# A two-layer graph network on one core: the first phase in one fixed order, and its buffers and loads shifted

## The chip, the cores and the metric

The kernel runs on one core of one Trainium2 chip. The metric is the device time of one execution in microseconds, as the median of the runs shown. All data are 32-bit floats. The engines are named as in the profile: PE is TensorE (PEld its weight loads), DVE is VectorE, ACT is ScalarE, POOL is GpSimd; SP is SyncE, which computes nothing and issues DMAs. ACT can issue DMAs too.

## The reference

The input is x, 128 graphs of 128 nodes with 256 features, and adj, one 128 x 128 matrix per graph. Cut to what is computed:

```python
# layer 0
norm  = (adj.sum(-1) + 1e-6) ** -0.5
f_hom = adj @ ((x @ theta) * norm) * norm
gate  = sigmoid(x @ W_t + b_t)
x1    = layernorm(x + elu(gate * f_hom + (1 - gate) * (x @ W_h)))
# layer 1
h      = relu(bn1(conv1d(x1^T, conv1_w)))              # one tap
x_conv = relu(bn2(conv1d(h, conv2_w, pad=8)) + x1^T)^T # 17 taps along the nodes
s      = x1 @ w_se.T + b_se                            # 3 coordinates per node
A      = exp(-|s_n - s_m|^2)
x_nmp  = A @ relu(x1 @ w_msg.T + b_msg)
out    = layernorm(x1 + GRU([x_conv, x_nmp], x1))
```

## The kernel before, in words

The work has three phases. The first phase computes layer 0 and, along the way, the first convolution and its analysis into 136 coefficients per channel and graph. It also turns the 17 taps of conv2_w into the same coefficients. The second phase multiplies coefficients of h and of the taps (L740, L753), and the third computes the rest of layer 1, mostly the products of the GRU (L999). The change touches only the first phase.

The first phase goes over 64 tiles of J = 2 graphs, in rounds t = -1 to 63. In round t several tiles are in work at once: l1_turn transposes x1 of tile t-2 on TensorE (L305) and VectorE copies it into the tile x1T (L309); l0_project multiplies x of tile t with theta and W_h (f_ps, L341) and with W_t (gate_ps, L346); between the two graphs of it come l0_gate of tile t-1 (L381 to L384) and l1_analyse of tile t-3 (coef_ps, L431); l0_elu of tile t-1 (L390, L391, statistics) and l0_norm (x1, L292) follow; l1_front of tile t-2 is the first convolution (conv_ps, L411) and h (L415 to L419); l0_turn of tile t+1 makes xT (a VectorE transpose of xb, L315) and the row sums of adj (L321, L323); l0_mix of tile t is L367 and L372.

SyncE issues the round's DMAs: l1_store of tile t-2 (x1 to x1_d at L423, x1T to x1T_d at L424), load_x of tile t (L134), load of tile t+2 (four DMAs of xb at L122, one of adjT at L129), in rounds 2 to 8 two small DMAs into TL (leftover_table, L275), and then what belongs to the taps.

The taps come in two kinds of units. Of the 32 units of w_unit, each takes 4 x 17 taps, loaded by w_load in four DMAs (L141) into one of two wt buffers; TensorE makes four products (w_ps, L447), ScalarE copies them into four wo buffers (L451), and w_store (L456) sends them to w_d in the next round. The 19 units of v_unit take the leftover rows: v_load (L471) brings up to 119 rows into one of two vt buffers, one product (wl_ps, L478), one copy on VectorE (L482), and v_store (L489) in the next round. The dicts units and units_v (L530 to L532) say in which round a unit is: before, units of the first kind are in rounds 2, 3, 5, 7, 9 and so on to 63, and those of the second kind in even rounds from 10 to 62. The v_load of the unit after next is issued at the end of the unit's own round.

What sets the order: manual_schedule(engines=...) keeps the instructions of the named engines in the order in which the code issues them; for the other engines a planner chooses the order from the dependencies and its own estimates. Before, each round has a manual_schedule of its own (L537): for TensorE alone up to t = 2, and for TensorE, SyncE, VectorE and ScalarE from t = 3 on. The end of the phase (L605 to L634) has another one. Tiles of one tag in a pool take turns in its buffers: x1T has one, x1, x, xb, hom, het and gate have two, adjT has four, xT one. An instruction that writes into a buffer waits until all that used the buffer's former tile is done, DMAs included.

At the start (L144 to L170) SyncE loads tile 0 and a third of w0 (the three weights of layer 0), and ScalarE issues the other two thirds, b_t, and eight small loads of the batch norms' vectors. Each third takes four DMAs of 64 KB. WARM = 7 matmuls without use (L529) run on TensorE before the first tile comes. VectorE computes a table of cosines (L209 to L223) in the rounds 0 and 1, and TensorE's program waits in places for VectorE there.

Of the kernel before, what the change touches and what calls it, by code (L numbers as in the profile page):

```python
# [26 lines left out]
M = L  # L27
# [7 lines left out]
def gnn_layers_kernel(ctx: ExitStack, tc: tile.TileContext, a: dict, out: bass.AP):  # L35
# [10 lines left out]
    nc = tc.nc  # L46
    x, adjT = a["x"], a["adjT"]
    NB = x.shape[0]
    NP = NB // J
# [43 lines left out]
    conv1_w = acon.tile([P, NC, D + CO], F32, tag="conv1_w", name="conv1_w")  # L93
    shift1 = acon.tile([P, D], F32, tag="shift1", name="shift1")
    K, Q = 32, P // 32
    WARM = 7
    NW = 2
    vt = [taps.tile([P, 2, D], F32, tag=f"vt{i}", name=f"vt{i}") for i in range(2)]
    wt = [taps.tile([P, 2, D], F32, tag=f"wt{i}", name=f"wt{i}") for i in range(NW)]


# [34 lines left out]
    NU = QF = P // Q  # L136

    def w_load(u):
        v = a["conv2_wT"].rearrange("(c f) t o -> f t c o", c=NC)
        for r in range(Q):  # L140
            nc.sync.dma_start(wt[u % NW][K * r : K * r + TAPS], v[r * QF + u])  # L141
# [112 lines left out]
    def way_back():  # L254

        AL = setup.tile([P, P // ML, ML], F32, tag="AL", name="AL")
        nc.vector.tensor_copy(AL, A[:, P:M].unsqueeze(1).to_broadcast([P, P // ML, ML]))
        nc.vector.memset(TL, 0.0)

        for t in vt:  # L260
            nc.vector.memset(t[96:], 0.0)
# [207 lines left out]
    def v_load(v):  # L469
        f, n = v_set(v)  # L470
        nc.sync.dma_start(  # L471
            vt[v % 2][0 : n * TAPS],
            a["conv2_wT"].rearrange("(c f) t o -> (f t) c o", c=NC)[f * TAPS : (f + n) * TAPS],
        )

    def v_unit(v):
        pl = bank(f"wl_ps_{v}")
        nc.tensor.matmul(  # L478
            pl, lhsT=TL, rhs=vt[v % 2].rearrange("p c o -> p (c o)"), start=True, stop=True
        )  # L480
        ol = s_v[v] = taps.tile([ML * FS, NC * D], F32, tag="wl", name=f"wl_o_{v}")
        nc.vector.tensor_copy(ol, pl[0 : ML * FS])  # L482
# [44 lines left out]
    warm = bank("warm_ps")  # L527
    for _ in range(WARM):
        nc.tensor.matmul(warm[:, 0:P], lhsT=ones, rhs=ones, start=True, stop=True)  # L529
    units = {2 + u * (NP - 3) // (NU - 1): u for u in range(NU)}  # L530
    rest = [t for t in range(3 + FS, NP - 1) if t not in units]
    units_v = {rest[v * (len(rest) - 1) // (NV - 1)]: v for v in range(NV)}  # L532
    hstack = ExitStack()
    H = None
    E = mybir.EngineType
    for t in range(-1, NP):
        with tc.manual_schedule(engines={E.PE, E.SP, E.DVE, E.Activation} if t > 2 else {E.PE}):  # L537

            def on(q, work):
                if 0 <= q < NP:  # L540
                    work(q)

            def between():
                on(t - 1, l0_gate)
                on(t - 3, l1_analyse)

            def beside():
                on(t - 1, l0_elu)

            on(t - 2, l1_turn)  # L550
            l0_project(t, between, beside) if t >= 0 else between()
            on(t - 1, l0_norm)
            if t == 0:
                norms = batch_norms()
                next(norms)
                l0_turn(1)
                table(AT2, (node, lag))

                cos, sin = T[:, 2:M:2], T[:, 3:M:2]
                both = setup.tile([P, M // 2 - 1], F32, tag="both", name="both")  # L560
                nc.vector.tensor_sub(both, sin, cos)
                nc.vector.scalar_tensor_tensor(sin, sin, -1.0, cos, ALU.mult, ALU.subtract)
                nc.vector.tensor_copy(cos, both)
            on(t - 2, l1_front)
            on(t - 2, l1_store)
            if t >= 0:
                load_x(t)
            if t + 2 < NP:
                if 2 <= t + 2:
                    load(t + 2)  # L570
                if 0 <= t < 2:
                    w_load(t)
                if 2 <= t < 2 + FS:
                    leftover_table(t - 2)
                if FS <= t < 2 + FS:
                    v_load(t - FS)
            else:
                m_load(t + 2 - NP)
            if t - 1 in units:
                w_store(units[t - 1])  # L580
                if units[t - 1] + NW < NU:
                    w_load(units[t - 1] + NW)
            if t - 1 in units_v:
                v_store(units_v[t - 1])
            if t != 0:
                on(t + 1, l0_turn)
            if t == 3:
                nc.scalar.dma_start(w_msg, a["w_msgT"].rearrange("(c p) e -> p c e", p=P))
                nc.scalar.dma_start(b_msg, a["L1_gnn_b_msg"].partition_broadcast(P))
            if t == 1:  # L590
                next(norms, None)
                way_back()
                sctx.close()
                hpool = hstack.enter_context(tc.tile_pool(name="hpool", bufs=1))
                H = hpool.tile([P, NC, M, NB], F32, tag="H", name="H")
            on(t, l0_mix)
            if t in units_v:
                v_unit(units_v[t])
                if units_v[t] + 2 < NV:
                    v_load(units_v[t] + 2)  # L600
            if t in units:
                if t + 1 < NP:
                    w_unit(units[t])
# [511 lines left out]
```

## Time and profile before

| what | value |
|---|---|
| median of 3 runs | 2004.11 us (2003.17 to 2006.05) |
| the profiled execution: its own time | 2004.55 us |
| its span, first to last instruction | 2002.8 us |
| first phase | from 0 to about 691 us |
| second and third phase | about 691 to 875 us, 875 us to the end |
| TensorE busy | 1974.8 us of the span |
| granted TensorE clock, mean | 0.994 |

A line of the table of stretches gives the stretch in us from the span's start, its length, and each engine's busy time and number of instructions in it, then the granted clock, the mean busy share of the 16 DMA engines and GB/s. A line of a timeline gives start, duration, engine, line of the code, operation, what it writes and reads, its shape and number; in brackets stands how long the engine was idle just before, and what ended that. Engine names with a q (SPq, ACTq) are the engine's issuing part; the duration of a DMA there is that of its issue, not of the transfer. When a transfer has landed is read from the record of the semaphore that it raises.

### The profile page before, as it was taken

How to read it: one execution, taken by the hardware profiler on the slowest of the kernel's cores; microseconds unless marked ns; L12 is line 12 of the kernel's file. 1: busy time of each engine (PE TensorE's matmuls, PEld its weight loads, DVE VectorE, ACT ScalarE, POOL GpSimd, SP SyncE). 2: the span in 40 equal slices, each digit the busy share in tenths (PEclk: the TensorE clock that was granted, in tenths of full speed). 3: DMA queues.
4: the chain of work that ended last, by engine and by line, in shares of the span. 5: the costliest groups of instructions: out<-in, count | busy, mean ns of one | idle time of the engine just before them, and what ended most of it. 6: DMA issues, size and time to landing. Idle time of an engine off the chain costs nothing.

```text
span 2002.8 us, 26505 instructions
## 1 busy us (share of the span) xinstructions
PE 1974.8 (99%) x8437; PEld 1348.1 (67%) x8437; DVE 1447.2 (72%) x2867; ACT 746.7 (37%) x1488; POOL 630.5 (31%) x855
## 2 busy tenths in 40 slices
PE   8999999999999999999999999999999999999997
PEld 5566666666666788876666666666666666666664
DVE  7678888888888654467777777767767776776766
ACT  3566666666666511122232222322222222222222
POOL 2111111111111255544243243424334343433331
PEclk9899999999999999999999999999999999999999
DMA  4566555566565689983212122212222221221100
GB/s 120 173 195 189 181 184 184 186 187 195 177 191 181 219 315 329 324 267 91 66 62 81 59 67 67 81 58 70 75 65 64 70 81 48 80 76 37 46 23 21
DMA packets 239568, 259.72 MB, mean 130 GB/s; under 512 B 84406, under 2 KB 174278, under 8 KB 239430
## 3 DMA queue, kind: packets, MB, share of 16 engines
q1 hardware_dynamic: 232982, 252.26, 39.3%
q10 hardware_dynamic: 6448, 5.78, 1.0%
q8 instruction: 68, 1.11, 0.2%
q14 instruction: 70, 0.57, 0.1%
HBM read 153.10 MB, written 104.86 MB: 129 GB/s over the span
## 4 chain that ended last, share of the span: by engine, by line
PE 94%; DVE 3%; DMA 1%; ACT 1%; issue 0%; POOL 0%; SPq 0%; ACTq 0%; POOLq 0%; DVEq 0%
PE g_ps L999 43%; PE f_ps L341 10%; PE y_ps L740 5%; PE msg_ps L876 5%; PE conv_ps L411 5%; PE gate_ps L346 5%; PE nmp_ps L932 3%; PE conv_ps L840 3%; PE coef_ps L431 3%; PE z_ps L753 3%; PE mix_ps L367 3%; PE x1T_ps L305 2%; PE w_ps L447 2%; PE conv_ps L847 1%; PE wl_ps L478 1%; PE adj_ps L321 1%
## 5 line engine op out<-in xcount | busy, mean ns | idle before, releaser
L341 PE MATMUL f_ps<-w,xT 128*128 128x512 f32 x512 | 246.3, 604 | 2.7 <-DVE xT L315 2.7
L174 POOL TENSOR_SCALAR rstd_b<-mv_b 128x2 f32<-128x2 f32 (+1 forms) x65 | 12.6, 194 | 529.5 <-DVE mv_b L283 529.5
L958 ACT ACTIVATE o<-o 128x1024 f32<-128x1024 f32 (+1 forms) x65 | 67.8, 1044 | 268.1 <-DVE o L1035 263.6
L999 PE MATMUL g_ps<-t_h,sh 128*128 128x384 f32 x384 | 156.9, 490 | 0.0
L999 PE MATMUL g_ps<-t_c,sc 128*128 128x384 f32 x384 | 155.3, 486 | 0.0
L999 PE MATMUL g_ps<-t_m,sm 128*128 128x384 f32 x384 | 155.3, 486 | 0.0
L292 ACT ACTIVATE y<-y,nb_b,rstd_b 128x256 f32<-128x256 f32 x128 | 70.0, 593 | 219.3 <-DVE nb_b L290 219.3
L346 PEld LDWEIGHTS gate_ps<-w,xT 128*128 128x128 f32 x512 | 98.4, 192 | 69.6 <-issue 61.9
L174 POOL TENSOR_SCALAR rstd_a<-mv_a 128x2 f32<-128x2 f32 x64 | 12.3, 192 | 400.7 <-DVE mv_a L283 400.7
L341 PEld LDWEIGHTS f_ps<-w,xT 128*128 128x128 f32 x512 | 89.5, 194 | 66.5 <-issue 66.4
L346 PE MATMUL gate_ps<-w,xT 128*128 128x256 f32 x512 | 132.6, 382 | 0.0
L1032 POOL TENSOR_TENSOR u<-u,p 128x512 f32<-128x512 f32 x63 | 79.9, 1267 | 162.7 <-DVE p L1016 162.7
L740 PE MATMUL y_ps<-wb,H 128*128 128x256 f32 x544 | 128.4, 379 | 0.8 <-issue 0.8
L411 PE MATMUL conv_ps<-conv_w,x1T 128*128 128x259 f32 x512 | 122.5, 381 | 0.0
L748 POOL TENSOR_TENSOR ws<-wb 128x512 f32<-128x512 f32 x67 | 92.5, 1381 | 89.7 <-PE z_ps L753 50.3
L350 ACT ACTIVATE hom<-f_ps,norm 128x256 f32<-128x256 f32 x128 | 60.7, 474 | 158.7 <-PE f_ps L341 158.7
L740 PEld LDWEIGHTS y_ps<-wb,H 128*128 128x128 f32 x544 | 103.3, 190 | 15.0 <-POOL ws L748 1.0
L876 PE MATMUL msg_ps<-w_msg,cx1T 128*128 128x256 f32 x480 | 108.7, 379 | 0.0
L999 PEld LDWEIGHTS g_ps<-t_c,sc 128*128 128x128 f32 x384 | 73.0, 190 | 50.9
L999 PEld LDWEIGHTS g_ps<-t_m,sm 128*128 128x128 f32 x384 | 73.0, 190 | 50.9
L411 PEld LDWEIGHTS conv_ps<-conv_w,x1T 128*128 128x128 f32 x512 | 97.1, 190 | 14.7 <-ACT w_o L451 0.2
L999 PE MATMUL g_ps<-w_hhT_w,cx1T 128*128 128x384 f32 x256 | 105.1, 492 | 0.0
(217 smaller groups left out, 4431.6 us busy)
## 6 DMA issues: line engine op xcount, KB each, us to landing
wb<-w_d SPq DMA_DIRECT2D x68, 512.0 KB
w_d<-w_o SPq DMA_DIRECT2D x128, 256.0 KB
y_d<-yb SPq DMA_DIRECT2D x68, 256.0 KB
xb<-in_x SPq DMA_DIRECT2D x256, 64.0 KB
x<-in_x SPq DMA_DIRECT2D x64, 256.0 KB
cx1T<-x1T_d SPq DMA_DIRECT2D x64, 256.0 KB
yt<-y_d SPq DMA_DIRECT2D x32, 512.0 KB
cx<-x_d SPq DMA_DIRECT2D x32, 512.0 KB
```

Of the source, the lines that this page charges most:

```text
L292: nc.scalar.activation(dst[:, q, :], src[:, q, :], AF.Identity, bias=nb[:, q : q + 1], scale=rstd[:, q : q + 1],)
L341: nc.tensor.matmul(pf, lhsT=xT[:, c, nodes(j)], rhs=w0[:, c, 0 : 2 * D], start=(c == 0), stop=(c == NC - 1),)
L346: nc.tensor.matmul(pg[:, j * D : (j + 1) * D], lhsT=xT[:, c, nodes(j)], rhs=w0[:, c, 2 * D : 3 * D], start=(c == 0), stop=(c == NC - 1),)
L350: nc.scalar.activation(hom[:, j, :], pf[:, 0:D], AF.Copy, scale=norm[:, j : j + 1])
L367: nc.tensor.matmul(pm[:, j * D : (j + 1) * D], lhsT=adjT_[:, j, :], rhs=hom[:, j, :], start=True, stop=True,)
L411: nc.tensor.matmul(ph[:, 0 : D + CO], lhsT=s["x1T"][:, c, nodes(j)], rhs=conv1_w[:, c, :], start=(c == 0), stop=(c == NC - 1),)
L740: nc.tensor.matmul(py[:, blk, :], lhsT=coefs(blk if k == 0 else 2 * k + 1 - blk, c), rhs=w[:, blk, c, :], start=(c == 0), stop=(c == NC - 1),)
L748: nc.gpsimd.tensor_tensor(ws, w[:, 0], w[:, 1], ALU.add)
L876: nc.tensor.matmul(pm[:, j * D : (j + 1) * D], lhsT=x1T[:, c, nodes(q)], rhs=w_msg[:, c, :], start=(c == 0), stop=(c == NC - 1),)
L958: nc.scalar.activation(rz, rz, AF.Tanh, scale=0.5)
L999: nc.tensor.matmul(pg[:, lo : lo + 3 * P], lhsT=s[f"f{kind}"][i][:, pr, :], rhs=factors[kind][i], start=(k == 0), stop=(k == 2), skip_grou ...
L1032: nc.gpsimd.tensor_tensor(u4, u2, p5, add)
```

## The change

- The rounds from t = 3 to 63 and the end of the phase stand in one manual_schedule for TensorE, SyncE, VectorE and ScalarE. The body of a round becomes a function, a_round. Rounds -1 to 2 stay as they were.
- x1T has two buffers instead of one, adjT three instead of four, vt one instead of two.
- v_load of the next unit is issued in the round after a unit, behind its v_store, and not two units ahead; v_load(1) in round 8 goes.
- w_load takes K = 32 consecutive rows for each of the four parts, where it took the 17 taps that are used; only the last part of the last unit takes 17. The products still read 17 rows.
- The units of the first kind are in rounds 2, 4, 6 to 32 and then 33, 35 to 63; the second kind goes to odd rounds from 11 to 31 and even rounds from 34 to 62.
- Each third of w0 comes in two DMAs of 128 KB over 128 partitions, not four of 64 KB over 32.
- WARM is 14. A small tanh on ScalarE (first) is issued after the first loads.

```diff
-    WARM = 7
+    WARM = 14
...
-    vt = [taps.tile([P, 2, D], F32, tag=f"vt{i}", name=f"vt{i}") for i in range(2)]
+    vt = taps.tile([P, 2, D], F32, tag="vt", name="vt")
...
-        s["adjT"] = io.tile([P, J, P], F32, tag="adjT", name=f"adjT_{p}")
+        s["adjT"] = io.tile([P, J, P], F32, tag="adjT", bufs=3, name=f"adjT_{p}")
...
-        v = a["conv2_wT"].rearrange("(c f) t o -> f t c o", c=NC)
+        v = a["conv2_wT"].rearrange("(c f) t o -> (f t) c o", c=NC)
         for r in range(Q):
-            nc.sync.dma_start(wt[u % NW][K * r : K * r + TAPS], v[r * QF + u])
+            n = TAPS if u == NU - 1 and r == Q - 1 else K
+            nc.sync.dma_start(wt[u % NW][K * r : K * r + n], v[(r * QF + u) * TAPS :][:n])
...
-        for q in range(Q):
-            (nc.sync if j == 2 else nc.scalar).dma_start(
-                w0[q * K : (q + 1) * K, :, j * D : (j + 1) * D],
-                a[name][2 * K * q : 2 * K * (q + 1)].rearrange("(c i) e -> i c e", i=K),
-            )
+        v = a[name].rearrange("(q c i) e -> c q i e", q=Q, c=NC)
+        for c in range(NC):
+            (nc.sync if j == 2 else nc.scalar).dma_start(w0[:, c, j * D : (j + 1) * D], v[c])
...
+    first = setup.tile([P, G], F32, tag="first", name="first")
+    nc.scalar.activation(first, neg_half, AF.Tanh)
...
-        s["x1T"] = wk.tile([P, NC, J * P], F32, tag="x1T", name=f"x1T_{p}")
+        s["x1T"] = wk.tile([P, NC, J * P], F32, tag="x1T", bufs=2, name=f"x1T_{p}")
...
-    units = {2 + u * (NP - 3) // (NU - 1): u for u in range(NU)}
+    units = {2 + 2 * u - 2 * u // NU: u for u in range(NU)}
...
-    for t in range(-1, NP):
-        with tc.manual_schedule(engines={E.PE, E.SP, E.DVE, E.Activation} if t > 2 else {E.PE}):
...
+    def a_round(t):
...
-            if FS <= t < 2 + FS:
-                v_load(t - FS)
+            if t == FS:
+                v_load(0)
...
         if t - 1 in units_v:
             v_store(units_v[t - 1])
+            if units_v[t - 1] + 1 < NV:
+                v_load(units_v[t - 1] + 1)
...
         if t in units_v:
             v_unit(units_v[t])
-            if units_v[t] + 2 < NV:
-                v_load(units_v[t] + 2)
...
+    for t in range(-1, 3):
+        with tc.manual_schedule(engines={E.PE}):
+            a_round(t)
     with tc.manual_schedule(engines={E.PE, E.SP, E.DVE, E.Activation}):
+        for t in range(3, NP):
+            a_round(t)
         last = NP - 1
```

More of the change, by code (lines that the diff above doesn't have):

```diff
@@ L258, in way_back @@
         nc.vector.memset(TL, 0.0)
-        for t in vt:
-            nc.vector.memset(t[96:], 0.0)
+        nc.vector.memset(vt[96:], 0.0)
         back = setup.tile([P, 1], F32, tag="back", name="back")
@@ L471, in v_load @@
         nc.sync.dma_start(
-            vt[v % 2][0 : n * TAPS],
+            vt[0 : n * TAPS],
             a["conv2_wT"].rearrange("(c f) t o -> (f t) c o", c=NC)[f * TAPS : (f + n) * TAPS],
@@ L478, in v_unit @@
         nc.tensor.matmul(
-            pl, lhsT=TL, rhs=vt[v % 2].rearrange("p c o -> p (c o)"), start=True, stop=True
+            pl, lhsT=TL, rhs=vt.rearrange("p c o -> p (c o)"), start=True, stop=True
         )
@@ L535, in gnn_layers_kernel @@
     E = mybir.EngineType
-    for t in range(-1, NP):
-        with tc.manual_schedule(engines={E.PE, E.SP, E.DVE, E.Activation} if t > 2 else {E.PE}):
[L539 to L574, printed above, removed]
-                if FS <= t < 2 + FS:
-                    v_load(t - FS)
[L577 to L598, printed above, removed]
-                if units_v[t] + 2 < NV:
-                    v_load(units_v[t] + 2)
-            if t in units:
-                if t + 1 < NP:
-                    w_unit(units[t])
@@ new lines, in gnn_layers_kernel, with on, between, beside @@
+    norms = batch_norms()
+    def a_round(t):
+        nonlocal H
+        def on(q, work):
+            if 0 <= q < NP:
+                work(q)
+        def between():
+            on(t - 1, l0_gate)
+            on(t - 3, l1_analyse)
+        def beside():
+            on(t - 1, l0_elu)
+        on(t - 2, l1_turn)
+        l0_project(t, between, beside) if t >= 0 else between()
+        on(t - 1, l0_norm)
+        if t == 0:
+            next(norms)
+            l0_turn(1)
+            table(AT2, (node, lag))
+            cos, sin = T[:, 2:M:2], T[:, 3:M:2]
+            both = setup.tile([P, M // 2 - 1], F32, tag="both", name="both")
+            nc.vector.tensor_sub(both, sin, cos)
+            nc.vector.scalar_tensor_tensor(sin, sin, -1.0, cos, ALU.mult, ALU.subtract)
+            nc.vector.tensor_copy(cos, both)
+        on(t - 2, l1_front)
+        on(t - 2, l1_store)
+        if t >= 0:
+            load_x(t)
+        if t + 2 < NP:
+            if 2 <= t + 2:
+                load(t + 2)
+            if 0 <= t < 2:
+                w_load(t)
+            if 2 <= t < 2 + FS:
+                leftover_table(t - 2)
+            if t == FS:
+                v_load(0)
+        else:
+            m_load(t + 2 - NP)
+        if t - 1 in units:
+            w_store(units[t - 1])
+            if units[t - 1] + NW < NU:
+                w_load(units[t - 1] + NW)
+        if t - 1 in units_v:
+            v_store(units_v[t - 1])
+            if units_v[t - 1] + 1 < NV:
+                v_load(units_v[t - 1] + 1)
+        if t != 0:
+            on(t + 1, l0_turn)
+        if t == 3:
+            nc.scalar.dma_start(w_msg, a["w_msgT"].rearrange("(c p) e -> p c e", p=P))
+            nc.scalar.dma_start(b_msg, a["L1_gnn_b_msg"].partition_broadcast(P))
+        if t == 1:
+            next(norms, None)
+            way_back()
+            sctx.close()
+            hpool = hstack.enter_context(tc.tile_pool(name="hpool", bufs=1))
+            H = hpool.tile([P, NC, M, NB], F32, tag="H", name="H")
+        on(t, l0_mix)
+        if t in units_v:
+            v_unit(units_v[t])
+        if t in units:
+            if t + 1 < NP:
+                w_unit(units[t])
```

## The prediction

> **What bounds the kernel now.** I read the busy shares first, then a table by stretches of 20 us, then the chain, the TensorE timeline and VectorE's and SyncE's around the places where TensorE is not full. The shares:
>
> ```profile
> PE 1974.8 (99%) x8437; PEld 1348.1 (67%) x8437; DVE 1447.2 (72%) x2867; ACT 746.7 (37%) x1488; POOL 630.5 (31%) x855
> ```
>
> TensorE is busy 99% of the span, so a change that leaves its work alone can win only where it idles or runs at half clock. The stretches (columns: busy us of PE, PEld, DVE, ACT, POOL with counts, granted clock, DMA share, GB/s) say where that is:
>
> ```profile
> 0.00:20.00 20.00, 13.52 (x41) 8.67 (x42) 14.18 (x49) 3.41 (x6) 5.33 (x21) 0.87 0.56 135
> 20.00:40.00 20.00, 18.32 (x70) 10.83 (x70) 15.50 (x39) 8.67 (x20) 3.05 (x9) 0.96 0.37 104
> 60.00:80.00 20.00, 18.34 (x73) 11.43 (x73) 9.30 (x22) 9.39 (x24) 2.67 (x6) 0.91 0.51 156
> 80.00:100.00 20.00, 17.31 (x64) 11.36 (x62) 14.53 (x34) 9.66 (x24) 2.67 (x6) 0.83 0.58 179
> 100.00:120.00 20.00, 20.00 (x97) 13.90 (x96) 16.14 (x38) 12.66 (x31) 3.56 (x8) 1.00 0.62 190
> ```
>
> From 100 to 680 us every stretch is 20.00 busy at clock 1.00: nothing to win there. Between 60 and 100 us TensorE gets through 73 and 64 matmuls instead of some 93, in part at a reduced clock. A round begins with the transposes into x1T_ps (L305); round 4 does so at 50.20, rounds 5 to 10 here:
>
> ```profile
> 59.85 0.33 PE L305 MATMUL x1T_ps<-ident,x 128*128 128x128 f32 x1
> ...
> 73.61 1.12 PE L305 MATMUL x1T_ps<-ident,x 128*128 128x128 f32 x4 [0.82 <-ACT coords L418]
> ...
> 87.37 1.39 PE L305 MATMUL x1T_ps<-ident,x 128*128 128x128 f32 x4 [2.67 <-ACT x L292]
> ...
> 101.06 0.65 PE L305 MATMUL x1T_ps<-ident,x 128*128 128x128 f32 x4
> ...
> 110.48 0.60 PE L305 MATMUL x1T_ps<-ident,x 128*128 128x128 f32 x4
> ...
> 121.00 0.66 PE L305 MATMUL x1T_ps<-ident,x 128*128 128x128 f32 x4
> ```
>
> An undisturbed round takes 9.42 us (101.06 to 110.48), with a unit of taps 10.52 (110.48 to 121.00). Rounds 5, 6 and 7 take 13.76, 13.76 and 13.69. The next two views say why:
>
> ```profile
> 65.25 0.69 DVE L309 COPY x1T<-x1T_ps 128x512 f32<-128x512 f32 x1 [4.38 <-DMA x1T_d<-x1T]
> ...
> 79.56 0.69 DVE L309 COPY x1T<-x1T_ps 128x512 f32<-128x512 f32 x1 [4.82 <-DMA x1T_d<-x1T]
> ```
>
> ```profile
> 54.57 1.99 SPq L141 DMA_DIRECT2D wt<-in_conv_wT  x4
> 56.66 0.80 SPq L423 DMA_DIRECT2D x_d<-x  x1
> 57.55 1.15 SPq L424 DMA_DIRECT2D x1T_d<-x1T  x1
> ```
>
> There is one x1T buffer. VectorE's copy into it, the first of its list in a round, stands until the previous tile's store has landed, with everything behind it. That store is late twice over. It is issued at 57.55, 7.4 us into the round, since SyncE stood 5.7 us ahead of the first w_store (L456): each DMA reports on one of eight semaphores taken in turn, its issue waits until the DMA before on that one has landed, and here that was the w_msg load, issued at 48.62. Then it lands only at 65.16 by the semaphore's record, 7.6 us after issue, where the same store issued at 41.03, with no loads of taps ahead of it, took 2.0. The four loads of taps ahead, 17 partitions each, land 1.5 to 1.7 us apart (59.13, 60.71, 62.39, 63.90), while the DMA engines are nearly empty:
>
> ```profile
> 59.30:60.50 1.20, 0.81 (x4) 0.21 (x2) 1.20 (x4) 1.20 (x4) 0.19 (x1) 1.00 0.82 241
> ...
> 77.00:78.00 1.00, 1.00 (x5) 0.76 (x4) 0.00 (x0) 0.56 (x2) 0.00 (x0) 1.00 0.14 39
> ```
>
> The first line is a stretch with a store under way, the second one in which such a load of taps is at the head: share 0.14, 39 GB/s.
>
> **The change, part by part.**
>
> *Second x1T buffer.* The copy in round t then needs the store of round t-2. For round 5 that is the one issued at 41.03, landed by 43.05; for round 6 the one landed at 65.16, where the copy would come at about 71. Both waits go.
>
> *Loads of taps with 32 rows.* The nearest row for 32 partitions is xb: its four loads of 64 KB, issued at 73.44 to 76.79 behind the taps, land 0.2 apart (80.28, 80.46, 80.70, 80.94). Four loads of taps, now 64 KB each, should so take about 1 us at the head of the queue instead of 6.4; issuing costs 0.45 each (xb's row) instead of 0.31 to 0.43. The surplus rows are 30 KB x 127 = 3.8 MB over 680 us, in which the queue moves over 120 MB: nothing. [...]
>
> *What of this lies on the path.* Rounds 4 to 7 (50.20 to 101.06) take 50.86 us; two plain and two with a unit would take 2 x 9.42 + 2 x 10.52 = 39.88. The excess, 10.98, holds the two waits, the half clock that follows them (f_ps at 88.56: 3.62 us for four where 1.88 is usual) and the waits for x1 at 87.37. What is late next: SyncE is still 6 us behind after the wait for w_msg, which I expect to stay. But round 4's list is now short (unit 1 moves from round 3 to 4, so its w_store and w_load, 4.85 us of issues, go to round 5), so SyncE ends round 4's issues near 62, where round 5 begins near 60. The x tile of round 4, issued near 58, lands by 61 and is needed by L390 near 64. So I take all: **-11.0**. Bounds: 0 (a new wait takes all of it) and -11.4 (round 3's 0.44 too).
>
> *Fewer loads at first.* Twelve loads of w0 become six. The adjT load is issued at 4.38 after 0.7 of waiting for a semaphore that a load of w0 holds, and the last xb load at 3.39 in place of 2.15. With half the loads, xb should land near 4.8 instead of 5.69 and adjT near 6.1 instead of 7.04. From there VectorE's list, full up to 15, leads to xT (17.86) and the second tile's f_ps (18.71): **-0.9**. Bounds: SyncE, VectorE and ScalarE are still placed by the planner in rounds -1 to 2, and it may place them otherwise; VectorE idles some 5 us between 15 and 39 (1.05 before 17.1, 1.53 before 23.6, 1.10 before 27.6, 0.70 before 34.1, 0.79 before 38.4), so from +2 to -4.
>
> *WARM 14.* The seven are 14 passes of 0.213 us from 1.12. Another 14 end by 1.12 + 28 x 0.213 = 7.1, and adj_ps now starts at 7.17, so they delay nothing. The granted clock is full at 4.68 to 8.09, half to 11.51, then full; with no idle time from 4.5 to 7.2 it should stay full, and the first tile's eight f_ps and eight gate_ps matmuls, 7.0 us from 7.56, take 5.2. But the second tile waits for VectorE (2.66 idle before 18.71): 0. [...]
>
> *Tanh at first* (1.28 us of table loading at 10.88 moves ahead): hom is ready earlier, but mix_ps stands behind gate_ps in TensorE's order until 15.02: 0.
>
> *One fixed order from the fourth round.* VectorE's, SyncE's and TensorE's lists of rounds 4 to 62 already follow the code, ScalarE's too but for unit 1's copies (L451), which drift into round 4 and wait there for w_store. With unit 1 in round 4 they have their buffers: 0. The new neighbours are units 15 and 16 in rounds 32 and 33: the four stores of 15 are issued up to 9.8 us into round 33 and land 2.4 to 4.5 later; unit 16's copies follow at about 10.6 to 12.1. ScalarE may wait up to 2 us, with mix_ps, which needs its hom, 8 us off: 0, bounds 0 and +2.
>
> *One vt buffer.* v_load moves from its unit's round to the next, behind v_store: issued about 8 us into a round of 10, it has 11 us until the next unit (the end of the round after, at the earliest). It lands after 4.7 to 5.0 us early on, 8.65 (median) later behind loads of taps, which now pass faster: 0. *Three adjT buffers*: the load waits for mix_ps of the round before, over when SyncE gets there: 0. *Later phases*: their code is the same; buffers lie elsewhere and TensorE's gaps at 680 to 875 us (3.5 in 195) may shift: 0, bounds -1 and +2.
>
> Sum: -11.0 - 0.9 = -11.9. The profiled execution took 2004.55 (span 2002.8 and 1.75 around it), 0.44 above the median; 2004.11 - 11.9 gives **1992.2 us**.
>
> **The rivals.**
>
> *Half of it stays* (14%). The x1T wait goes, but SyncE's lag makes x or x1 the late one: 2.16 of waiting at 93.59 and the 2.67 at 87.37 speak for such waits, the freed round-4 list against it. 5 to 6 us are won: 1998.
>
> *The start gives more* (12%). The first tile at full clock (7.0 - 5.2 = 1.8 us), or VectorE's xT placed nearer to 15 (3 us earlier): 2 to 4 more, 1988 to 1990. VectorE's full list speaks against.
>
> *The wait moves and nothing is won* (7%): 2001 to 2006. It would need another transfer as slow as the loads of taps ahead of each round; none is in the records.
>
> *The wider loads stay as narrow* (5%, the slower side). Were a load's time set by its bytes alone, 64 KB would take 1.6 x 64/34 = 3.0 us, four 12 us. The x load behind them would land near 15 us after its round's start, L390 needs it at 9.4 + 3.9 = 13.3: some 1.7 us in each of about 31 rounds, so 2045 or more. It decides once the four take over 10.8 us. Against it: xb's 64 KB land 0.2 apart.
>
> **How the numbers follow.** Forecast 62%, the rest as given. 0.2% (4 us, about what a measurement of this kernel can tell from no change; its three runs spread over 2.9) puts faster below 2000.1: 62 + 14 + 12 = 88%; same 7%, slower 5%. The forecast's own range is 1990 to 1996. The 80% range takes in half of it staying and half of the better starts, 62 + 14 + 6 = 82%: **1987 to 1999**.
>
> **What the changed profile would show.** Stretches 60 to 100 at 19.9 or more of 20 and clock 1.00; rounds 5 to 7 of 9.4 to 10.6 us; no VectorE wait for x1T_d in the first 130 us; SyncE's waits for loads of taps, 50.4 us at L122, nearly gone; the second tile's f_ps near 17.8. I am wrong if a new wait stands ahead of L390 or L292 in rounds 4 to 8, or if the rounds after 100 us grow past 10.6.

## The result

The changed kernel takes 1998.92 us (median of 8 runs, 1997.64 to 1999.80); the kernel before, measured beside it, 2004.58 (8 runs, 2003.17 to 2006.05). The ratio is 0.997, 95% interval 0.9959 to 0.9981: 5.7 us faster. The forecast was 1992.2 us, 11.9 less than before. The direction is right and the time lies inside the range, but less than half of the forecast gain came. The profiled execution took 1999.04 us (span 1997.1).

### The profile page after: what moved, and what is told of

Same layout as the page of the kernel before. It is cut to its first block, busy times and chain, and to the rows that moved or that the text cites. A ratio compares the mean times of both kernels' runs of the same rounds, so it can differ in the third digit from the quotient of the medians.

```text
span 1997.1 us, 26580 instructions
## 1 busy us (share of the span) xinstructions
PE 1971.5 (99%) x8451; PEld 1348.2 (68%) x8451; DVE 1448.3 (73%) x2866; ACT 747.0 (37%) x1489; POOL 630.3 (32%) x855
## 4 chain that ended last, share of the span: by engine, by line
PE 95%; DVE 2%; DMA 1%; ACT 0%; issue 0%; POOL 0%; SPq 0%; POOLq 0%; DVEq 0%; ACTq 0%
PE g_ps L1007 43%; PE f_ps L343 11%; PE conv_ps L413 5%; PE y_ps L748 5%; PE gate_ps L348 5%; PE msg_ps L884 5%; PE coef_ps L433 3%; PE nmp_ps L940 3%; PE conv_ps L848 3%; PE z_ps L761 3%; PE mix_ps L369 3%; PE x1T_ps L307 2%; PE w_ps L449 2%; PE conv_ps L855 1%; PE wl_ps L480 1%; PE adj_ps L323 1%
```

## The profile after

TensorE's busy share is the same:

```profile
PE 1971.5 (99%) x8451; PEld 1348.2 (68%) x8451; DVE 1448.3 (73%) x2866; ACT 747.0 (37%) x1489; POOL 630.3 (32%) x855
```

The table of stretches of the changed kernel (busy us of PE, PEld, DVE, ACT, POOL with counts, granted clock, DMA share, GB/s):

```profile
0.00:20.00 20.00, 13.05 (x43) 8.81 (x44) 9.97 (x31) 2.23 (x4) 3.23 (x17) 0.83 0.44 114
20.00:40.00 20.00, 16.70 (x56) 9.69 (x55) 15.25 (x43) 6.40 (x15) 3.88 (x8) 0.91 0.48 131
60.00:80.00 20.00, 20.00 (x93) 13.84 (x92) 16.22 (x37) 12.94 (x30) 3.55 (x8) 1.00 0.78 236
80.00:100.00 20.00, 20.00 (x94) 13.89 (x93) 16.18 (x37) 12.95 (x30) 3.55 (x8) 1.00 0.64 195
```

From 60 to 100 us TensorE is now busy throughout, at full clock, with 93 and 94 matmuls where there were 73 and 64: the stall of rounds 4 to 7 is gone. But the first two lines have become worse. VectorE is busy 9.97 us of the first 20 where it was 14.18, TensorE 16.70 of the next 20 where it was 18.32, and the clock is 0.83 and 0.91 where it was 0.87 and 0.96.

The starts of rounds 5 to 10 on TensorE's timeline:

```profile
64.93 0.66 PE L307 MATMUL x1T_ps<-ident,x 128*128 128x128 f32 x4
...
74.34 0.60 PE L307 MATMUL x1T_ps<-ident,x 128*128 128x128 f32 x4
...
84.87 0.66 PE L307 MATMUL x1T_ps<-ident,x 128*128 128x128 f32 x4
...
94.28 0.60 PE L307 MATMUL x1T_ps<-ident,x 128*128 128x128 f32 x4
...
104.81 0.66 PE L307 MATMUL x1T_ps<-ident,x 128*128 128x128 f32 x4
...
114.22 0.60 PE L307 MATMUL x1T_ps<-ident,x 128*128 128x128 f32 x4
```

Rounds 5 to 9 take 9.41 or 10.53 us, without a wait in brackets. From the start of round 3 to that of round 10 it is 69.59 us (44.63 to 114.22) where it was 81.76 (39.24 to 121.00). One unit of taps, 1.10 us, has moved out of this stretch, so the stall was worth 81.76 - 69.59 - 1.10 = 11.07. VectorE's copy waits for TensorE alone, 0.61 us:

```profile
65.62 0.69 DVE L311 COPY x1T<-x1T_ps 128x512 f32<-128x512 f32 x1 [0.61 <-PE x1T_ps L307]
```

SyncE's list shows the loads of taps and the stores behind them (start of the issue, its duration):

```profile
59.47 2.37 SPq L143 DMA_DIRECT2D wt<-in_conv_wT  x4
61.94 0.37 SPq L425 DMA_DIRECT2D x_d<-x  x1
62.40 0.38 SPq L426 DMA_DIRECT2D x1T_d<-x1T  x1
```

By their semaphores' records the four loads land at 62.09, 62.27, 62.53 and 63.39, some 0.2 apart but for the last, which was issued 0.9 after the third. The store of x1T issued at 62.40 lands at 65.25, 2.9 us later where the one behind the narrow loads took 7.6.

The same records say how the narrow loads did that. A DMA raises its semaphore in steps. Leaving out the step that comes as the issue ends, a load of 17 rows has a single step, at its landing; a load of 32 rows has sixteen, and so has the store. Of the sixteen steps of the store issued at 57.55 before the change, fifteen came by 60.39 and the last one at 65.16. From 26.9 to 28.4 us before the change only loads of 17 rows were under way, and the DMA share was 0.07, 1.1 of 16 engines, at 25 GB/s. So I read a step as the part of one DMA engine, though the records do not name the engines: one engine did the four narrow loads one after the other, and one sixteenth of the store stood behind them.

What took the gain back lies ahead of round 3, which begins at 44.63 instead of 39.24, +5.39. TensorE's timeline at the start, before and after:

```profile
1.12 3.35 PE L529 MATMUL warm_ps<-ones 128*128 128x128 f32 x14 [1.12 <-POOL ones L73]
7.17 0.41 PE L321 MATMUL adj_ps<-ident,adjT 128*128 128x128 f32 x2 [2.70 <-DMA adjT<-in_adjT]
...
18.71 3.46 PE L341 MATMUL f_ps<-w,xT 128*128 128x512 f32 x4 [2.66 <-DVE xT L315]
...
28.47 0.33 PE L305 MATMUL x1T_ps<-ident,x 128*128 128x128 f32 x1 [0.70 <-ACT x L292]
...
39.24 0.33 PE L305 MATMUL x1T_ps<-ident,x 128*128 128x128 f32 x1 [0.66 <-ACT x L292]
```

```profile
1.12 5.66 PE L531 MATMUL warm_ps<-ones 128*128 128x128 f32 x28 [1.12 <-POOL ones L73]
11.19 0.66 PE L323 MATMUL adj_ps<-ident,adjT 128*128 128x128 f32 x2 [4.42 <-DMA adjT<-in_adjT]
11.64 3.62 PE L343 MATMUL f_ps<-w,xT 128*128 128x512 f32 x4
...
17.65 0.70 PE L348 MATMUL gate_ps<-w,xT 128*128 128x256 f32 x2 [1.12 <-DMA w<-in_L_gnn_W_t]
...
22.50 1.95 PE L343 MATMUL f_ps<-w,xT 128*128 128x512 f32 x4 [0.18 <-DVE xT L317]
...
33.15 1.39 PE L307 MATMUL x1T_ps<-ident,x 128*128 128x128 f32 x4 [3.09 <-ACT x L294]
34.33 3.02 PE L343 MATMUL f_ps<-w,xT 128*128 128x512 f32 x4
...
44.63 1.01 PE L307 MATMUL x1T_ps<-ident,x 128*128 128x128 f32 x4
```

TensorE now waits for DMAs, 4.42 us for the first matrix (adjT) and 1.12 for W_t, and in round 2 it waits 3.09 us for x1, which ScalarE writes. VectorE's first transpose, before and after:

```profile
5.71 0.71 DVE L315 STREAM_TRANSPOSE xT<-xb 128x512 f32<-128x512 f32 x1 [2.49 <-DMA xb<-in_x]
```

```profile
10.68 0.71 DVE L317 STREAM_TRANSPOSE xT<-xb 128x512 f32<-128x512 f32 x1 [7.54 <-DMA xb<-in_x]
```

The delay is 4.97 us at xT, 4.02 at adj_ps, 3.79 at the second tile's f_ps, 4.68 at round 2 and 5.39 at round 3; the last part of it is half clock at 34.33 (f_ps 3.02 where 1.88 is usual). So -11.07 + 5.39 = -5.7. The spans of the two profiled executions, 2002.8 and 1997.1, differ by as much: the rest of the kernel gives nothing.

The loads at the start, on ScalarE's and SyncE's lists of the changed kernel:

```profile
0.72 1.74 ACTq L151 DMA_DIRECT2D w<-in_L_gnn_theta  x2
2.49 1.10 ACTq L151 DMA_DIRECT2D w<-in_L_gnn_W_h  x2
```

```profile
0.72 4.83 SPq L122 DMA_DIRECT2D xb<-in_x  x4
6.99 0.35 SPq L129 DMA_DIRECT2D adjT<-in_adjT  x1
10.93 1.34 SPq L151 DMA_DIRECT2D w<-in_L_gnn_W_t  x2
```

The two halves of theta land at 5.24 and 7.67, those of W_h at 8.94 and 10.37, those of W_t at 15.52 and 17.60: 1.3 to 2.4 us apart for 128 KB each. The four loads of xb, issued between them, land at 2.54, 5.22, 6.98 and 10.58; before, they had landed by 5.69. Two stretches in which such a load is at the head, in the columns of the table of stretches:

```profile
9.00:10.20 1.20, 0.00 (x0) 0.00 (x0) 0.00 (x0) 0.00 (x0) 0.00 (x0) 0.63 0.24 75
13.00:14.20 1.20, 1.20 (x2) 0.34 (x1) 1.10 (x4) 0.17 (x1) 0.80 (x1) 0.50 0.26 76
```

The DMA share is 0.24 and 0.26, about a quarter of 16 engines, at 75 GB/s; 128 KB at that rate are 1.7 us. The semaphores say it more plainly. A half of theta has four steps at its landing (4.88, 5.02, 5.03, 5.24), where each of the twelve loads of before has sixteen. The xb load issued at 1.18 has sixteen steps: twelve come by 3.76, the other four at 4.84 to 5.22. By the reading above that is the picture of the narrow loads of taps again, with four engines instead of one: they carry the new loads, and a quarter of the xb load stands behind them.

## Experiments on the start

Three theories: the new loads run on four engines, since the view that they read, "(q c i) e -> c q i e", has q = 4 as its slowest dimension; or 128 KB in one load is the trouble whatever the engines; or the planner places the first rounds otherwise for another reason (14 warming matmuls, the tanh, fewer loads).

**The changed kernel with the twelve old loads.**

```diff
-        v = a[name].rearrange("(q c i) e -> c q i e", q=Q, c=NC)
-        for c in range(NC):
-            (...).dma_start(w0[:, c, j * D : (j + 1) * D], v[c])
+        for q in range(Q):
+            (...).dma_start(
+                w0[q * K : (q + 1) * K, :, j * D : (j + 1) * D],
+                a[name][2 * K * q : 2 * K * (q + 1)].rearrange("(c i) e -> i c e", i=K),
+            )
```

> The changed kernel with the twelve loads of w0 of the kernel before. Theory of the engines: each of the new loads runs on four DMA engines, since the slowest dimension of its source has four entries, and all that queues behind it waits; with the old loads the xb tile lands by 5.7 us as before, round 2 begins near 28 us instead of 33.2, and the time is 1993.5 us (1992 to 1995). Theory of the size: loads of 128 KB are slow whatever their pattern; the same number here. Theory of the planner: the start is longer because the planner has ordered it otherwise (WARM, the tanh, the small loads); the time stays near 1999.

Measured: 1994.11 us (1993.70 to 1995.07), ratio to before 0.9954 (0.9942 to 0.9967). The last xb lands at 5.39, adjT at 6.93, and round 3 begins at 40.62 instead of 44.63. Against the kernel before it wins 9.4 us instead of 5.7, so 3.8 come back, and 4.0 by the start of round 3: the loss is in these loads. (The intervals of the two ratios touch, but no run of either kernel lies among those of the other, and the next experiment shows the loss by itself.) Round 3 still begins 1.4 us later than before. TensorE's timeline shows that, and besides what the 14 warming matmuls do:

```profile
7.49 1.96 PE L345 MATMUL f_ps<-w,xT 128*128 128x512 f32 x4
...
13.43 1.03 PE L371 MATMUL mix_ps<-hom,adjT 128*128 128x256 f32 x4
18.61 3.75 PE L345 MATMUL f_ps<-w,xT 128*128 128x512 f32 x4 [4.16 <-DVE xT L319]
```

The first tile runs at full clock (f_ps 1.96 for four, 3.23 before) and mix_ps begins at 13.43 instead of 15.02. But the second tile waits for VectorE, 4.16 us instead of 2.66, begins at 18.61 instead of 18.71, and is at half clock for longer. By the record of the granted clock, half of full speed was granted for 3.4 us at the first tile and 3.4 at the second before, and here for 6.8 from 17.98, all at the second. So round 2 begins at 29.86 instead of 28.47.

**The new loads alone, put into the kernel before.**

> The kernel before with the six new loads of w0 alone. Theories of the engines and of the size: the start loses what it loses in the changed kernel, 2004.6 + 5 = 2009.6 us (2007 to 2012), with the first xb landing near 10.5 us. Theory of the planner: 2004.6 us as before.

Measured: 2007.81 us (2006.22 to 2008.85), ratio 1.0021 (1.0012 to 1.003): 4.3 us slower with nothing else changed. xb lands at 10.36; VectorE's and TensorE's timelines:

```profile
10.46 0.71 DVE L313 STREAM_TRANSPOSE xT<-xb 128x512 f32<-128x512 f32 x1 [7.24 <-DMA xb<-in_x]
```

```profile
45.35 1.01 PE L303 MATMUL x1T_ps<-ident,x 128*128 128x128 f32 x4
```

Round 3 begins at 45.35, 0.7 us after that of the changed kernel, with 7 warming matmuls and without the tanh, so neither of them is needed for it. It begins 6.1 us later than before, but 1.8 of the stall go in turn (9.27 us of it are left), so that 4.3 remain at round 10.

**Six loads of the same size with another view.** Row 2p + c of each weight matrix goes to partition p instead of rows 64q + 32c + i, and xT is read in the matching order. A load is 128 KB as in the changed kernel, but the slowest dimension of its source is 128.

```diff
-        v = a[name].rearrange("(q c i) e -> c q i e", q=Q, c=NC)
+        v = a[name].rearrange("(p c) e -> c p e", c=NC)
...
-            s["xb"].rearrange("p b (c i) -> p c b i", c=NC),
+            s["xb"].rearrange("p b (i c) -> p c b i", c=NC),
```

> The changed kernel with six loads of w0 as large as now (128 KB, 128 partitions, pieces of 1 KB), but row 2p+c of a weight on partition p, so that the slowest dimension of the source has 128 entries; the transpose of xb reads every second element to match. Theory of the engines: the six loads pass quickly, xb lands by 5.7 us, the time is 1993 us (1991 to 1995). Theory of the size: as slow as the changed kernel, 1999 us. Theory of the planner: 1999 us too. If the transpose of xb gets slower than 0.71 us by its stride, that shows in its row.

Measured: 1993.39 us (1992.32 to 1994.34), ratio 0.9949 (0.9936 to 0.9961). The halves of theta and W_h land at 3.65, 4.32, 4.88 and 5.20, 0.3 to 0.7 apart, and round 3 begins at 40.36:

```profile
6.85 0.71 DVE L317 STREAM_TRANSPOSE xT<-xb 128x512 f32<-128x512 f32 x1 [3.70 <-DMA xb<-in_x]
```

Same number of loads, same bytes in each, another slowest dimension, and each of the six now has sixteen steps at its semaphore: the size falls as a cause, and so does a planner upset by fewer loads; the four engines (0.24 and 0.26 of 16, against 0.74 here from 3.0 to 5.5 us) stand. Note that xb lands at 6.75, later than with twelve loads (5.39). The prediction had it come forward with half the loads, and it did not: the loads of 128 KB are under way beside xb, and the third xb load is still issued only at 3.88, when the DMA before on its semaphore, the first xb load, has landed (3.87).

**Three loads of 256 KB.** The same view, both halves in one load ("(p c) e -> p c e").

> As the kernel with six linear loads, but one load of 256 KB per weight (pieces of 2 KB). Theory of the engines: three issues fewer, 1992.5 us (1990 to 1995). Theory of the size: slower than the changed kernel, 2000 us or more.

Measured: 1993.48 us (1992.67 to 1994.37), ratio 0.995 (0.9938 to 0.9963). The last xb lands at 7.99, since b_t and the small loads of the batch norms' vectors now come sooner in the turn of eight semaphores: it shares one with b_t, which lands at 6.24, and is issued at 6.26. Round 3 begins at 39.33. The time does not differ from that with six.

**The small loads behind.** Three loads of 256 KB, and b_t and the eight small loads on SyncE's queue behind the loads of tile 1.

```diff
+    load(1)
...
-        nc.scalar.dma_start(t, a[name][lo:hi].partition_broadcast(P))
+        nc.sync.dma_start(t, a[name][lo:hi].partition_broadcast(P))
...
-            nc.scalar.dma_start(
+            nc.sync.dma_start(
...
-    load(1)
```

> The kernel with three linear loads of w0 (1993.5 us), with b_t and the eight small loads of the batch norms' vectors moved from ScalarE's queue to SyncE's, behind the loads of tile 1. If the start is set by how many DMAs take a turn on the eight semaphores ahead of xb and adjT, xb is complete near 5 us instead of 8.0, adjT near 6 instead of 8.8, TensorE reaches round 3 near 37 instead of 39.3, and the time is 1990 to 1992 us. If VectorE's own list (the table of cosines, full up to some 15 us) sets round 3, xb comes early and the time stays within 1 us of 1993.5.

Measured: 1994.19 us (1992.55 to 1995.33), ratio 0.9954 (0.9942 to 0.9967). xb lands at 6.17 and adjT at 6.51, 1.8 and 2.3 us sooner than with the small loads ahead, and TensorE's timeline shows where it goes:

```profile
15.80 2.93 PE L343 MATMUL f_ps<-w,xT 128*128 128x512 f32 x4 [1.91 <-DVE xT L317]
...
27.87 0.33 PE L307 MATMUL x1T_ps<-ident,x 128*128 128x128 f32 x1 [2.79 <-ACT x L294]
```

The second tile begins 2.6 us sooner (18.40 with the small loads ahead), but round 2 waits 2.79 for its x1; round 3 begins at 38.62, 0.7 sooner, and the time does not show it. So the loads were late by their turn, as the first theory has it, but the time goes by the second: something behind them sets round 3. The wait is for x1, at the end of VectorE's and ScalarE's lists; which instruction there holds it was not tried.

**Seven warming matmuls.** The kernel with the old loads, WARM = 7.

> The changed kernel with the old twelve loads of w0 (1994.1 us) and 7 instead of 14 warming matmuls. If the warming is worth nothing, as predicted, 1994 us within 1 us, and round 3 begins at 40.6 us as with 14. If it decides which windows of the clock are full, the first tile runs at half clock as in the kernel before (half from 8.09 to 11.51 us) and the time moves by 1 to 2 us either way.

Measured: 1993.81 us (1993.13 to 1993.88), ratio 0.9953 (0.9939 to 0.9966), where 14 gave 0.9954. In this execution the second tile is at full clock (f_ps 1.95 us for four) and round 3 begins at 38.60, 2.0 us sooner than with 14; at the end of the span 0.8 of it is left (1991.5 against 1992.3). WARM is worth nothing that can be measured.

## Experiments on the stall

The prediction gave -11.0 to the second x1T buffer and the 32-row loads together. These runs take them apart, with the moved units as a third part. To compare them I take the time from the start of round 3 to that of round 10, less 69.59 us, or 70.69 where four units of taps lie in these rounds and not three.

**Before with two x1T buffers** (and, to make room, one vt buffer with its loads in the round after a unit, as in the change).

> The kernel before with two x1T buffers; one vt buffer with its loads in the round after a unit, to make room. Theory that either remedy of the stall in rounds 5 to 7 is enough: the wait of VectorE for x1T_d goes, rounds 5 to 7 come down from 13.7 to 10.5 us or less, 1993 to 1995 us. Rival, half of it stays: the loads of taps still hold up x and x1, rounds 5 to 7 keep a part of their excess, 1996 to 2000 us.

Measured: 2001.52 us (1999.76 to 2002.91), ratio 0.9989 (0.9979 to 0.9998). Waits of VectorE from 50 to 105 us (total, times, longest), and the stretches:

```profile
DVE gate L389 <- DMA x<-in_x: 7.1, 2, 5.3
```

```profile
60.00:80.00 20.00, 19.28 (x88) 12.85 (x87) 11.87 (x26) 12.61 (x30) 2.67 (x6) 1.00 0.53 164
80.00:100.00 20.00, 16.66 (x65) 10.24 (x64) 14.35 (x34) 8.99 (x22) 3.56 (x8) 0.83 0.58 180
```

The copy no longer waits for a store, but four instructions behind it in VectorE's list the tile x is late by the same queue: it is the next load behind the narrow ones. 8.00 of 11.07 us stay. That is the rival "half of it stays", here in a purer form than it was told.

**Before with 32-row loads of taps.**

```diff
-        v = a["conv2_wT"].rearrange("(c f) t o -> f t c o", c=NC)
+        v = a["conv2_wT"].rearrange("(c f) t o -> (f t) c o", c=NC)
...
-            nc.sync.dma_start(wt[u % NW][K * r : K * r + TAPS], v[r * QF + u])
+            n = TAPS if u == NU - 1 and r == Q - 1 else K
+            nc.sync.dma_start(wt[u % NW][K * r : K * r + n], v[(r * QF + u) * TAPS :][:n])
```

> The kernel before with loads of taps of 32 rows alone, one x1T buffer. Theory that either remedy is enough: the x1T store lands 2 to 3 us after its issue in place of 7, before the next copy, rounds 5 to 7 come down to 10.6 us or less, 1993 to 1995 us. Rival: the store is issued too late anyway (the wait for w_msg), the copy still waits some 2 us in rounds 5 and 6, 1996 to 2000 us. Start in rounds 0 to 2 as before, or up to 0.5 us shorter.

Measured: 1994.99 us (1993.57 to 1997.54), ratio 0.9959 (0.9944 to 0.9973). 1.24 us of the stall stay, with one x1T buffer and no wait for its store. Most of them are in round 5, which takes 11.44 us where 10.52 is usual and waits for ScalarE's coords, TensorE's line first and then ScalarE's list. Copies of unit 1 (L453) have drifted into round 4 and stand between the work that leads to it:

```profile
61.39 0.55 PE L307 MATMUL x1T_ps<-ident,x 128*128 128x128 f32 x3 [0.65 <-ACT coords L420]
```

```profile
58.81 1.07 ACT L453 ACTIVATE w_o<-w_ps 128x512 f32<-128x512 f32 x2
59.77 0.60 ACT L294 ACTIVATE x<-hom,nb_a,rstd_a 128x256 f32<-128x256 f32 x1
60.26 0.59 ACT L453 ACTIVATE w_o<-w_ps 128x512 f32<-128x512 f32 x1
60.74 0.60 ACT L294 ACTIVATE x<-hom,nb_a,rstd_a 128x256 f32<-128x256 f32 x1
61.23 0.24 ACT L420 ACTIVATE coords<-conv_ps 128x3 f32<-128x3 f32 x2
```

**The changed kernel with one x1T buffer.**

> The changed kernel with one x1T buffer again. Theory that either remedy is enough: 1999 us as the changed kernel, no VectorE wait for x1T_d above 1 us. Rival: some 2 us of waits in rounds 4 to 6, 2001 to 2003 us.

Measured: 1997.88 us (1996.95 to 2000.33), ratio 0.9974 (0.9965 to 0.9983), where the changed kernel has 0.997 (0.9959 to 0.9981): the same, and no stall. Beside the wide loads the second buffer is worth nothing.

**The changed kernel with 17-row loads.**

> The changed kernel with loads of taps of 17 rows again, two x1T buffers. Theory that either remedy is enough: 1999 us as the changed kernel; SyncE's waits for loads of taps at L122 are back (some 50 us) and cost nothing. Rival: late x tiles cost 2 to 5 us, 2001 to 2004 us.

Measured: 2001.34 us (1998.71 to 2003.48), ratio 0.9989 (0.9979 to 0.9998). 2.61 us of stall, again with x late (VectorE's waits from 50 to 105 us):

```profile
DVE gate L390 <- DMA x<-in_x: 3.1, 1, 3.1
```

With two x1T buffers and 17 rows this kernel stalls much less than the kernel before does with the same two (8.00). What differs is above all the units, and the later start, which took 1.8 off the stall in the run with the new loads of w0 alone; the next two kernels take the units by themselves.

**Before with the units moved, and nothing else.** (The units of the second kind follow, since they take rounds that the first kind leaves free.)

```diff
-    units = {2 + u * (NP - 3) // (NU - 1): u for u in range(NU)}
+    units = {2 + 2 * u - 2 * u // NU: u for u in range(NU)}
```

> The kernel before with nothing but the units of taps moved: loads of 17 rows, one x1T buffer. If the narrow loads alone are the cause, as the run of before with 32 rows says, the stall only moves to the rounds after the units: rounds of 12 us and more remain and the time is 2002 to 2004. If it takes units in neighbouring rounds (2 and 3) for the queue to fall behind, rounds 5 to 7 shrink to 9.4 to 11 us as in the changed kernel with 17 rows, and the time is 1996 to 1998.

Measured: 1999.85 us (1998.31 to 2001.99), ratio 0.9982 (0.9973 to 0.999). 5.60 us of stall stay, and one wait for the store of x1T instead of two:

```profile
64.42 0.69 DVE L309 COPY x1T<-x1T_ps 128x512 f32<-128x512 f32 x1 [5.02 <-DMA x1T_d<-x1T]
...
73.83 0.68 DVE L309 COPY x1T<-x1T_ps 128x512 f32<-128x512 f32 x1
```

With units in rounds 2 and 3 the loads of two units are issued in rounds 3 and 4, one after the other; with units in 2 and 4, in rounds 3 and 5, with a round between in which the queue empties: the store of x1T issued there at 66.15 lands 2.5 us later. Neither expectation fits: the stall neither moves on nor goes, it is halved.

**Before with 32 rows and the units moved.**

> The kernel before with the loads of 32 rows and with the units of taps moved (2, 4, 6 to 32, 33, 35 to 63), one x1T buffer and all the rest as it was. If these two make the whole gain after the start, rounds 5 to 8 take 9.4 and 10.5 us, round 5 loses the 1 to 2 us that it kept with the 32 rows alone (11.44 us there), and the time is 993 to 994 us above 1000, that is 1993 to 1994. If the second x1T buffer or the fixed order is needed for them, round 5 stays at 11.4 and the time at 1995.

Measured: 1993.66 us (1993.62 to 1997.18), ratio 0.9955 (0.9942 to 0.9969). Nothing of the stall stays, in rounds of 9.41 and 10.52 us:

```profile
60.00:80.00 20.00, 20.00 (x96) 13.84 (x92) 16.15 (x37) 12.94 (x30) 3.57 (x9) 1.00 0.76 221
80.00:100.00 20.00, 20.00 (x96) 13.84 (x92) 16.18 (x37) 12.93 (x30) 3.61 (x9) 1.00 0.64 196
```

This kernel, two edits of the change, is 9.7 us faster than the one before, where the whole change wins 5.7; the intervals of the two ratios still touch (0.9942 to 0.9969 and 0.9959 to 0.9981). The kernels with linear loads (0.9949 and 0.995) can't be told from it.

**The changed kernel with a schedule of its own for each round from the third on.**

> The changed kernel with a schedule of its own for each round from the third on, as before, in place of the one for all of them. If the one fixed order is worth nothing, as predicted, 1998.9 us within 1 us and the same rounds (9.41 and 10.53 us). If it is what takes the stall away, rounds 5 to 7 grow again by 2 us or more each.

Measured: 1998.34 us (1995.80 to 1999.41), ratio 0.9975 (0.9966 to 0.9983); rounds 5 to 10 take 9.42 and 10.52. The one fixed order is worth nothing.

The runs side by side:

| kernel | taps' rows | x1T | units | round 3 begins | stall in rounds 3 to 9 | median less that of before |
|---|---|---|---|---|---|---|
| before | 17 | 1 | old | 39.24 | 11.07 | |
| two x1T | 17 | 2 | old | 39.92 | 8.00 | -2.1 |
| units moved | 17 | 1 | moved | 38.99 | 5.60 | -3.5 |
| 32 rows | 32 | 1 | old | 39.81 | 1.24 | -8.7 |
| 32 rows, units moved | 32 | 1 | moved | 39.80 | 0.03 | -9.7 |
| after | 32 | 2 | moved | 44.63 | 0 | -5.7 |
| after, one x1T | 32 | 1 | moved | 45.65 | 0 | -5.8 |
| after, 17 rows | 17 | 2 | moved | 45.38 | 2.61 | -2.3 |
| after, old loads of w0 | 32 | 2 | moved | 40.62 | 0 | -9.4 |
| after, six linear loads of w0 | 32 | 2 | moved | 40.36 | 0 | -10.1 |
| before, new loads of w0 | 17 | 1 | old | 45.35 | 9.27 | +4.3 |

Each stall is from one profiled execution, each median from several, and the two need not agree to 2 us: the executions of one kernel lie up to 5 us apart. So the moved units alone are worth 5.5 us by the trace and 3.5 by the medians.

## Why the prediction was wrong, step by step

- **What bounds the kernel, and the place of the stall: right.** The excess of rounds 4 to 7 went, and the rest of the kernel takes what it took.
- **-11.0 for the stall: the sum was right (11.07 in the trace), its parts were not.** The step put the two waits for x1T_d down to the single buffer and the slow loads alike and took both remedies. By the traces the wide loads are worth 9.8 by themselves and the moved units the remaining 1.2; the second buffer, worth 3.1 by itself, wins nothing beside them (alone, by the medians: 8.7, 3.5 and 2.1). The buffer is where the delay showed, the queue is where it came from. The step did name the moved unit as what lets SyncE catch up, which the run with it alone bears out.
- **The wide loads' time: right.** About 1 us for four was expected, and they land within 1.3 us, 0.2 to 0.3 apart but for the one issued late.
- **"Fewer loads at first", -0.9, bounds +2 to -4: this is the step that failed.** The loads cost 3.8 us by the medians when they are taken out of the changed kernel and 4.3 when they are put alone into the one before; of the +5.39 at round 3 in the trace, 4.0 go with them; the other 1.4 stayed with the old loads, and the medians do not show it. The last xb load, forecast near 4.8, landed at 10.58, adjT at 11.05 instead of 6.1, and the second tile's f_ps, forecast near 17.8, began at 22.50. The step counted loads and turns on the eight semaphores, and took it for granted that a load over 128 partitions is at least as fast as one over 32. xb's row, from which it drew, is a load of 32 partitions from 32 rows. The destination's 128 partitions hide that the source is a view whose slowest dimension has 4 entries, and that is the side that counts here: four steps at the semaphore, a share of 0.24 to 0.26 of 16 engines and landings 1.3 to 2.4 us apart, where the view with 128 entries outermost gave sixteen steps and landings 0.3 to 0.7 apart with the same bytes. The prediction asked for the taps how the access is cut up, and not for this load, the other one that the change alters.
- **The bounds of that step** came from placement alone (+2). A bound from the nearest rows was at hand in the same trace: the loads of taps, 1.6 us for 34 KB each at a share of 0.07, about one engine of 16, were slow by the form of the access and not by their bytes (xb's 64 KB landed 0.2 apart), and nothing excluded that for a new view.
- **WARM 14, tanh, the fixed order: 0, right for the time.** In the changed kernel itself the first tile ran at half clock (f_ps 3.62 us), after TensorE had waited 4.42 us for adjT. With the old loads it went to full clock as the rival "the start gives more" had it, and the second tile waited for VectorE all the same (4.16 us), as the step said. That the clock stays full without idle time was an estimate from the trace of before, where 2.70 us of idle time up to 7.17 came ahead of half clock from 8.09. In the run with the old loads TensorE was idle for 1.03 us up to 7.07, the clock was granted in full from 4.3 us and at half from 17.98, and the first tile's f_ps took 1.96 us, 3.23 before; the time was VectorE's to give. The tanh was not tried alone. One vt and three adjT buffers: the kernel with the old loads has them, the one before with 32 rows and moved units has not, and they end within the spread (1994.1 and 1993.7).
- **The rivals.** None of them came true in the changed kernel. Its 1998.9 us sits on the time of "half of it stays" (1998), but no wait for x or x1 is left in rounds 4 to 8; a matching time is no evidence for a mechanism. That rival's mechanism did come in two of the experiments, both with 17 rows. "The wait moves" and "the wider loads stay as narrow" came nowhere. Neither of the two named signs of being wrong, a new wait ahead of L390 or L292 and longer rounds after 100 us, came either, since the loss lies ahead of those rounds. The rival that was missing is the other load, slower at the start by its view.
- **Readings that were off, with no weight in the sum.** The 2.16 us at 93.59 that "half of it stays" takes as a sign of a late x are a wait for ScalarE's gate (L384). And by the numbers beside it the four wide loads would begin to hold L390 at about 10.4 us, 12 less 1.7, not 10.8.

## What to carry to other kernels

For each DMA whose access is rewritten, look at how both sides are cut up, not only at the number of partitions on the chip's side: here the split "(q c i)", which puts 4 entries outermost, kept 0.24 to 0.26 of the 16 DMA engines busy, and what was queued behind it waited too (xb until 10.58 us instead of 5.69). The trace of a load shows it: here the steps of its semaphore were four, and sixteen with 128 entries outermost. Where a wait shows at a buffer, look first at what is ahead of that transfer in its queue: here a second buffer alone moved the wait to the next load in the line. Undo each part of a change alone, since a gain of 9.4 us and a loss of 3.8 in it look from outside like a gain of 5.7.

## What the runs showed of the hardware

- The number of steps with which a load raised its semaphore at its landing differed with the slowest dimension of its access: one for 17 rows (128 loads of taps before), seven for 119 rows (18 loads of v_load), sixteen for 32 rows (127 loads of taps after), four for the view with 4 entries outermost (6 loads of w0 after). With loads of one step alone under way the DMA share was 0.07 (26.9 to 28.4 us before), with a load of four steps at the head 0.24 and 0.26.
- Loads of four steps held up loads of sixteen. An xb load of 64 KB issued at 1.18 us landed at 5.22 beside a half of theta that landed at 5.24, and the one issued at 5.24 landed at 10.58, 0.2 after the last half of W_h; in both, twelve of the sixteen steps came some 1.5 to 2.2 us before the last. With the same bytes in loads of sixteen steps (six linear loads) xb was complete at 6.75.
- Three remedies for one stall, worth 3.1, 5.5 and 9.8 us alone by the traces (2.1, 3.5 and 8.7 by the medians), are worth 11.07 together, and the last two alone make 11.04.
- A first tile at full clock (f_ps 1.96 us against 3.23) came with a longer half clock at the second tile in that execution (6.8 us from 17.98, where before it was 3.4 at each of the two), and did not move the time: 1994.1 us with 14 warming matmuls, 1993.8 with seven.
